# Four graph-attention layers on one core: the last head's norm, scaling and output of a batch written into the next batch's layer 0

## The chip, the core and the metric

The kernel runs on one core of a Trainium2 chip. A core has TensorE (PE; its weight loads are shown apart as PEld), VectorE (DVE), ScalarE (ACT), GpSimd (POOL) and SyncE (SP), and 16 DMA engines that move data between the device memory and the on-chip memories SBUF and PSUM. The metric is the device time of one execution in microseconds (us).

## The reference, cut to what matters

There are 16 batches of 1024 nodes with 256 features, and one 0/1 adjacency matrix of 1024 x 1024 for each batch. Four layers follow one another, and each adds an attention over the graph to x:

```python
h = jnp.maximum(_layernorm(x, axis=-1), 0.0)
x = x + _L0_gnn_ref(h, adj, L0_gnn_W, L0_gnn_a)
...
h = jnp.maximum(_layernorm(x, axis=-1), 0.0)
x = x + _L3_gnn_ref(h, adj, L3_gnn_W, ...)
```

Layers 0 to 2 have one head of 256 features. Layer 3 has H = 4 heads of E = 64 features, and its end is what the change is about; per head and node it is

```python
dst = jnp.einsum('bhij,bhje->bhie', attention, h) + bias[None, :, None, :]
out = jax.nn.relu(dst) + h
mu = out.mean(axis=-1, keepdims=True)
var = out.var(axis=-1, keepdims=True)
out = (out - mu) / jnp.sqrt(var + EPS) * ln_gamma[None, :, None, :] + ln_beta[None, :, None, :]
```

and the four heads side by side are added to x, which is the output.

## The kernel before

**Layout.** A batch's x lies in one tile `x_b` of 128 partitions by 8 row blocks by 256 features. The attention weights of a layer or head are 8 tiles `weights` of 128 x 1024, each built by one VectorE instruction (L318 in `weigh`) from `row`, a PSUM tile that TensorE fills with 8 transposes (L314), and from the adjacency mask. `row` has one buffer for everybody: `weigh` waits in `row_taken` until the one before has built its 8 tiles.

**One layer (`attend`).** The 8 tiles of weights are built while TensorE makes the products (L409) of row blocks 0 and 1 into two PSUM accumulators `acc`. Then each further row block i of 2 to 7 takes 8 products. `finish` reads an accumulator, scales it by the inverse of the row's total (L333, L334) and adds it to x: L449 on VectorE in layer 0, and in layers 1 and 2 `add_elu` with L341 and L343 on ScalarE and L344 and L345 on VectorE. Every second block, `project` begins the next layer for a pair of blocks: mean and centring on VectorE (L271, L274), the squares on ScalarE (L281), the inverse root on GpSimd (L260, L261), the transposes on TensorE (L290), their copy `hT` on ScalarE (L292), the projection on TensorE (L297), and the eviction into `V` (L361, then L363 or L365; for layer 3 L381 and L382 into `h3`, then GpSimd's L384, L388 and L389).

**Layer 3.** For each of the four heads the products (L519) use quarter tiles of TensorE. The sums are copied by ScalarE (L581), transposed (L588, L596), divided by the totals and written to `y` (L599). Then two helpers follow: `center(h)` adds the bias on GpSimd (L487), applies relu and adds h3 (L488), takes the mean (L490, L491), subtracts it (L492), squares on ScalarE (L494), sums the squares (L496) and calls the inverse root on GpSimd (L260, L261); `rescale` multiplies by it on VectorE (L500) and by gamma on GpSimd (L501), and adds x (L502). A head's `rescale` is written behind the next head's L599; that of the last head stands at the end of the batch, with the two output DMAs (L613).

**Order.** The kernel is two Python generators, `stream(0)` over the even batches and `stream(1)` over the odd ones. Each `yield` hands back an estimated duration, and the stream with the smaller sum goes on; the second starts 111 units late, so that one stream is in layer 3 while the other is in layers 0 to 2. This gives the order in which instructions are written. The framework then orders each engine's instructions by that order and by readiness, except where `keep_in_program_order` pins one; it also places tiles in buffers and sets all semaphores. Of the tiles concerned, `y` and `h3` have one buffer for both streams, `x_b` three, `V` four, the accumulators two per stream.

Of the kernel before, what the change touches and what calls it, by code (L numbers as in the profile page):

```python
# [59 lines left out]
def short_path(ctx: ExitStack, tc: tile.TileContext, ins: dict, out: bass.AP, bad: bass.AP):  # L60

    nc = tc.nc
    x, adj = ins["x"], ins["adj"]
    B, N, D = x.shape
    H, T, E = ins["L3_a_src"].shape
    NI = N // P
    NK = D // P
    HALF = 512
    NH = N // HALF
    NG = HALF // P  # L70
# [25 lines left out]
    def in_blocks(a: bass.AP) -> bass.AP:  # L96
        return a.rearrange("(c p t) f -> p c t f", p=P, t=2)
# [166 lines left out]
    def accumulator(b: int) -> bass.AP:  # L264
        return psum.tile([P, HALF], F32, name=f"acc{b % 2}")
# [40 lines left out]
    def weigh(b: int, column, c, op, into: list):  # L306


        while row_taken:
            yield 0.25  # L310
        row_taken.append(b)
        r = psum.tile([P, N], F32, name="row", bufs=1)
        for i in range(NI):
            nc.tensor.transpose(r[:, ts(i, P)], column(i).to_broadcast([P, P]), ident)  # L314
        yield 0.5
        for j in range(NI):
            w = edges.tile([P, N], F32, name=f"weights{b % 2}")
            nc.vector.scalar_tensor_tensor(w, r, c(j), masks[b][:, j // 2, :, j % 2], op0=op, op1=ALU.mult)  # L318
            into.append(w)
            if j == NI - 1:  # L320
                row_taken.pop()
            yield 0.5

    def start(behind, b: int):

        for t in behind:
            if row_taken == [b]:
                return
            yield t
# [16 lines left out]
            xi, above, 0.0, xi, op0=ALU.add, op1=ALU.add, accum_out=total  # L346
        )

    def batch(b: int):
        xb = xs.pop(b)  # L350
        if b == 0:
            next(preparing)
# [40 lines left out]
        def attend(l: int, V: bass.AP, finish, then: int):  # L393

            weights = []
            behind = weigh(
                b, lambda i: V[:, i, D + 2 : D + 3], lambda j: V[:, j, D + 1 : D + 2],
                ALU.min if l == 1 else ALU.max, weights,
            )
            yield from start(behind, b)  # L400
            following = begin(then) if then < 3 else begin3()
            steps = iter(())
            accs = {}
            sums = small.tile([P, NI], F32, name="sums_of_x")

            def product(i: int, j: int):
                if j == 0:
                    accs[i] = accumulator(b)[:, : D + 1]
                nc.tensor.matmul(  # L409
                    accs[i], weights[j][:, ts(i, P)], V[:, j, : D + 1],  # L410
                    start=(j == 0), stop=(j == NI - 1),
                )


            for j in range(NI):
                next(behind)
                product(0, j)
                product(1, j)
                if b == 0 and j == NI - 1:


                    next(preparing)
                    if l == 0:
                        next(loading[1])
                    next(preparing, None)
                yield 0.9
            for _ in behind:
                pass
            for i in range(NI):
                if i > 1:  # L430
                    for j in range(NI):
                        product(i, j)
                acc = accs.pop(i)
                finish(i, acc, sums[:, i : i + 1])
                if i != 0:
                    yield 3.6
                if i % 2 == 1:

                    yield from steps
                    steps = project(b, then, xb, sums, i // 2, following[1])  # L440
                yield from islice(steps, 1)
            yield 1.0
            yield from steps
            return following[0]
# [9 lines left out]
        def finish(i: int, acc: bass.AP, total: bass.AP):  # L454
            add_elu(xb[:, i, :], acc, total)
# [23 lines left out]
        y = single.tile([P, NI, H, E], F32, name="y")  # L479
        normed = []  # L480
        shape = [P, NI, E]

        def center(h: int):

            yh = y[:, :, h, :]
            head = ts(h, E)
            nc.gpsimd.tensor_add(yh, yh, bias[:, head].unsqueeze(1).to_broadcast(shape))  # L487
            nc.vector.scalar_tensor_tensor(yh, yh, 0.0, h3[:, :, head], op0=ALU.max, op1=ALU.add)  # L488
            mean = small.tile([P, NI], F32, name="mean")
            nc.vector.tensor_reduce(mean, yh, AX.X, ALU.add)  # L490
            nc.vector.tensor_scalar_mul(mean, mean, 1.0 / E)  # L491
            nc.vector.tensor_sub(yh, yh, mean.unsqueeze(2).to_broadcast(shape))  # L492
            square = wide.tile(shape, F32, name="wide", bufs=1)
            nc.scalar.activation(square, yh, AF.Square)  # L494
            var = small.tile([P, NI], F32, name="var")
            nc.vector.tensor_reduce(var, square, AX.X, ALU.add)  # L496
            return yh, head, inverse_root(var, NI, E, L3_EPS)

        def rescale(yh: bass.AP, head, rstd: bass.AP):
            nc.vector.tensor_mul(yh, yh, rstd.unsqueeze(2).to_broadcast(shape))  # L500
            nc.gpsimd.tensor_mul(yh, yh, gamma[:, head].unsqueeze(1).to_broadcast(shape))  # L501
            nc.gpsimd.tensor_add(yh, yh, xb[:, :, head])  # L502
# [46 lines left out]
        for h in range(H):  # L549


            acc = accumulator(b)
            total = accumulator(b)
            if h == 0:
                for first in range(0, NI, 4):
                    for _ in range(4):
                        next(behind)
                    pinned = []
                    for j in (first + 2, first):
                        add_values(h, j)  # L560
                    yield 3.6
                for _ in behind:
                    pass
            behind = weigh3(h + 1)
            yield from start(behind, b)

            for first in range(0, NI, 4):
                pinned = []
                for j in (first + 2, first):
                    add_totals(h, j)  # L570
                    if h > 0:
                        add_values(h, j)
                for _ in range(4):
                    next(behind, None)
                yield 1.8 if h == 0 else 5.4
            for _ in behind:
                pass
            copies = []
            for accT in (acc, total) if h == 0 else (total, acc):
                copies.append(wide.tile([P, HALF], F32, name="sums"))  # L580
                nc.scalar.copy(copies[-1], accT)  # L581
                next(testing)
                next(coming, None)
            sums, totals = copies if h == 0 else copies[::-1]
            yield 0.5
            turned = psum.tile([P, NG, P], F32, name="misc")
            for i in range(NG):
                nc.tensor.transpose(turned[:, i, :], totals[:, ts(i, P)], ident)  # L588
            inv = small.tile([P, NH, NG], F32, name="inv8")
            nc.vector.tensor_reduce(  # L590
                inv, turned[:, :, ::QUAD].rearrange("p i (g n) -> p g i n", n=2), AX.X, ALU.add
            )
            inverse(inv, inv)
            turned = psum.tile([P, NG, NH, E], F32, name="misc")
            for i in range(NG):
                nc.tensor.transpose(  # L596
                    turned[:, i].rearrange("p g e -> p (g e)"), sums[:, ts(i, P)], ident
                )
            nc.vector.tensor_mul(  # L599
                y[:, :, h, :].rearrange("p (g i) e -> p g i e", g=NH),  # L600
                turned.rearrange("p i g e -> p g i e"),
                inv.unsqueeze(3).to_broadcast([P, NH, NG, E]),
            )
            yield 0.5
            if h > 0:
                rescale(*normed.pop())
            normed.append(center(h))
            yield 1.0
        for _ in coming:
            pass  # L610
        rescale(*normed.pop())
        for g in range(NH):
            nc.gpsimd.dma_start(  # L613
                in_blocks(out[b, ts(g, HALF), :]),
                y[:, ts(g, NG)].rearrange("p (c t) h e -> p c t (h e)", t=2),
            )
        yield 1.0


    def stream(first: int):  # L620
        for _ in loading[first]:
            yield 2.0
        for b in range(first, B, 2):
            yield from batch(b)

    loading, preparing = [load(0), load(1)], prepare()
    next(loading[0])
# [2 lines left out]
    while streams:  # L630
        ahead = min(streams, key=lambda s: s[0])
        t = next(ahead[1], None)
# [381 lines left out]
```

## Time and profile before

The time before is 2988.73 us, the median of three runs (2987.17 to 2989.75). The span of the profiled execution is 2988.9 us with 44636 instructions.

| what | busy us | share of the span |
|---|---|---|
| TensorE matmuls | 2839.7 | 95% |
| TensorE weight loads | 1986.1 | 66% |
| VectorE | 2148.9 | 72% |
| ScalarE | 1090.0 | 36% |
| GpSimd | 956.7 | 32% |

| group of instructions | count | busy us, mean ns of one |
|---|---|---|
| L409 PE products of layers 0 to 2 | 6144 | 1436.6, 385 |
| L519 PE products of layer 3 | 6144 | 692.1, 597 |
| L318 DVE weights (both forms) | 896 | 1104.2, 1273 and 1275 |
| L488 DVE relu and h3 | 64 | 44.2, 690 |
| L494 ACT squares of a head | 64 | 40.1, 627 |
| L487 POOL bias | 64 | 84.8, 1325 |
| L501 POOL gamma | 64 | 81.4, 1273 |
| L502 POOL adding x | 64 | 83.6, 1307 |
| L613 POOL output DMA issues | 32 | 24.8, 775 |

A matmul's mean of 385 ns is its stay in the pipeline and not the interval between two: a row of 32 of L409 takes 6.93 us. A bracket in a timeline, such as [1.16 <-POOL y L487], is the time for which the engine stood idle just before the instruction, and what ended it.[...]

### The profile page before, as it was taken

What the parts mean: (1) busy time and instruction counts of PE and PEld (TensorE: products, weight loads), DVE (VectorE), ACT (ScalarE), POOL (GpSimd) and SP (SyncE); (2) the same over time, 40 slices, a digit from 0 to 9 for tenths busy, and PEclk for the clock granted to TensorE, in tenths of its full rate; (3) what the DMA queues carried; (4) which work ended last, traced back from release to release, by engine and by line L of the source; (5) the groups of instructions that cost most, each with busy time, mean ns of one, the idle gap of its engine ahead of it and who ended that gap; (6) DMA issues with size and microseconds to landing.
All of it is one profiled execution on the core that took longest, in us unless ns stands there. A gap on an engine that the chain in (4) does not pass through costs nothing.

```text
span 2988.9 us, 44636 instructions
## 1 busy us (share of the span) xinstructions
PE 2839.7 (95%) x16774; PEld 1986.1 (66%) x16774; DVE 2148.9 (72%) x4467; ACT 1090.0 (36%) x3009; POOL 956.7 (32%) x1455
## 2 busy tenths in 40 slices
PE   7999999999999999999999999999999999999985
PEld 5775856768576685766758566685766857667552
DVE  5658688585976859678586885859768586785855
ACT  2333434343343433424334243433434334343331
POOL 2123324243242423424233242432424233242333
PEclk9999999999999999999999999999999999999987
DMA  7204122040221303122041220302213031110101
GB/s 122 39 8 60 33 29 57 8 50 29 30 56 17 55 16 50 36 29 57 5 51 32 29 57 8 50 29 32 55 17 59 11 50 36 15 29 6 25 18 26
DMA packets 120495, 106.11 MB, mean 36 GB/s; under 512 B 73680, under 2 KB 91216, under 8 KB 120272
## 3 DMA queue, kind: packets, MB, share of 16 engines
q0 software_dynamic: 40448, 67.12, 15.4%
q1 hardware_dynamic: 79824, 36.05, 5.8%
q8 instruction: 135, 2.21, 0.3%
q14 instruction: 88, 0.72, 0.1%
HBM read 153.49 MB, written 33.55 MB: 63 GB/s over the span
## 4 chain that ended last, share of the span: by engine, by line
PE 55%; DVE 28%; issue 8%; POOL 5%; ACT 3%; DMA 1%; POOLq 0%; SPq 0%; ACTq 0%; DVEq 0%
PE acc L409 33%; DVE weights L318 19%; PE acc L297 9%; PE acc L519 9%; PE misc L290 2%; POOL rstd L261 2%; POOL y L487 1%; ACT square L281 1%; DVE x_b L345 1%; DVE V L365 1%; PE row L314 1%; DVE x_b L344 1%; ACT below L341 1%; DVE y L488 1%; DVE var L496 1%
## 5 line engine op out<-in xcount | busy, mean ns | idle before, releaser
L409 PE MATMUL acc<-V,weights 128*128 128x257 f32 x6144 | 1436.6, 385 | 26.2 <-DVE weights L318 15.7
L409 PEld LDWEIGHTS acc<-V,weights 128*128 128x128 f32 x6144 | 1143.3, 191 | 262.0 <-DVE weights L318 68.5
L318 DVE SCALAR_TENSOR_TENSOR weights<-row,ex,mask 128x1024 f32<-128x1024 f32 x512 | 630.3, 1273 | 102.5 <-PE row L314 95.7
L519 PE MATMUL acc<-weights,V 128*32 128x512 f32 x6144 | 692.1, 597 | 11.4 <-DVE weights L318 7.5
L297 PE MATMUL acc<-W,hT 128*128 128x259 f32 (+1 forms) x2048 | 521.6, 391 | 40.4 <-ACT hT L292 28.9
L297 PEld LDWEIGHTS acc<-W,hT 128*128 128x128 f32 x2048 | 379.0, 191 | 148.3 <-ACT hT L292 35.1
L318 DVE SCALAR_TENSOR_TENSOR weights<-row,V,mask 128x1024 f32<-128x1024 f32 x384 | 473.9, 1275 | 0.7 <-PE row L314 0.7
L519 PEld LDWEIGHTS acc<-weights,V 128*32 128x32 f32 x6144 | 189.4, 110 | 422.9 <-issue 415.3
L341 ACT ACTIVATE below<-acc,inv 128x256 f32<-128x256 f32 x256 | 120.8, 472 | 798.9 <-DVE inv L334 559.5
L281 ACT ACTIVATE square<-x_b,minus_mean 128x256 bf16<-128x256 f32 x512 | 259.7, 507 | 230.8 <-DVE minus_mean L271 155.0
L261 POOL TENSOR_TENSOR rstd<-rstd,minus_half 128x2 f32<-128x2 f32 (+1 forms) x320 | 302.0, 944 | 20.3
L389 POOL TENSOR_TENSOR x_b<-x_b,beta 128x256 f32<-128x256 f32 x128 | 93.4, 730 | 490.9 <-ACT square L281 490.9
L260 POOL TENSOR_SCALAR rstd<-squared 128x2 f32<-128x2 f32 x256 | 57.7, 225 | 573.2 <-ACT square L281 572.3
L333 DVE TENSOR_SCALAR inv<-acc 128x1 f32<-128x1 f32 x256 | 39.3, 154 | 277.6 <-PE acc L409 276.4
L344 DVE SCALAR_TENSOR_TENSOR x_b<-below,x_b 128x256 f32<-128x256 f32 x256 | 136.8, 534 | 82.7 <-ACT below L341 82.5
L292 ACT ACTIVATE hT<-misc 128x512 f32<-128x512 f32 x256 | 150.0, 592 | 119.9 <-PE misc L290 119.5
L361 ACT ACTIVATE V<-acc,rstd 128x3 f32<-128x3 f32 x384 | 98.5, 262 | 251.7 <-PE acc L297 250.8
L581 ACT COPY sums<-acc 128x512 f32<-128x512 f32 x128 | 74.8, 585 | 278.6 <-PE acc L519 278.6
L365 DVE TENSOR_SCALAR V<-acc,rstd,V 128x256 f32<-128x256 f32 x256 | 131.7, 538 | 62.2 <-ACT V L361 61.3
L290 PE MATMUL misc<-ident,centered 128*128 128x128 f32 x1024 | 158.7, 277 | 15.7 <-DVE centered L274 13.9
L274 DVE TENSOR_SCALAR centered<-x_b,minus_mean 128x256 f32<-128x256 f32 x512 | 168.5, 357 | 5.2
L290 PEld LDWEIGHTS misc<-ident,centered 128*128 128x128 f32 x1024 | 121.3, 141 | 60.1 <-issue 26.9
(76 smaller groups left out, 2218.1 us busy)
## 6 DMA issues: line engine op xcount, KB each, us to landing
adj_i<-in_adj_dram POOLq DMA_DIRECT2D x128, 256.0 KB, 3.9
x_b<-in_x_dram SPq DMA_DIRECT2D x16, 1024.0 KB, 6.4
narrow<-in_adj_dram POOLq DMA_DIRECT2D x64, 256.0 KB, 9.3
out_dram<-y POOLq DMA_DIRECT2D x32, 512.0 KB, 7.4
mask<-narrow SPq DMA_TRANSPOSE x64, 4.4
W<-in_L_gnn_W_dram SPq DMA_DIRECT2D x3, 256.0 KB, 7.2
weights<-in_L_gnn_a_dram SPq DMA_DIRECT2D x3, 256.0 KB, 8.5
W<-in_L_gnn_W_dram SPq DMA_DIRECT2D x2, 128.0 KB, 8.2
```

Source lines behind the costliest of these rows:

```text
L261: nc.gpsimd.tensor_tensor(r, r, minus_half.to_broadcast([P, n]), op=ALU.pow)
L274: nc.vector.tensor_scalar(centered[:, n, :], xb[:, 2 * pair + n, :], minus_mean[:, n : n + 1], 0.0, op0=ALU.add, op1=ALU.max,)
L281: nc.scalar.activation(square, xb[:, 2 * pair + n, :], AF.Square, bias=minus_mean[:, n : n + 1], accum_out=squared[:, n : n + 1],)
L290: nc.tensor.transpose(turned[:, k, ts(n, P)], centered[:, n, ts(k, P)], ident)
L292: nc.scalar.mul(hT, turned, ROOT_D)
L297: nc.tensor.matmul(projected, hT[:, k, ts(n, P)], W[l][:, k, :], start=(k == 0), stop=(k == NK - 1),)
L318: nc.vector.scalar_tensor_tensor(w, r, c(j), masks[b][:, j // 2, :, j % 2], op0=op, op1=ALU.mult)
L341: nc.scalar.activation(below, acc[:, :D], AF.Exp, scale=inv)
L344: nc.vector.scalar_tensor_tensor(xi, below, 1.0, xi, op0=ALU.min, op1=ALU.add)
L365: nc.vector.tensor_scalar(V[:, i, :D], projected[:, :D], rstd, V[:, i, D : D + 1], op0=ALU.mult, op1=ALU.mult,)
L409: nc.tensor.matmul(accs[i], weights[j][:, ts(i, P)], V[:, j, : D + 1], start=(j == 0), stop=(j == NI - 1),)
L519: made = nc.tensor.matmul(accT[ts(n, QUAD), :], values, moving, start=first, stop=last)
```

## The change

`batch` becomes a generator that returns another generator, `ending`. It holds what was at the end of the batch: `center` of the last head, its `rescale`, and the two output DMAs, in three pieces. `stream` hands it to the next `batch` of the same stream, and layer 0's loop over row blocks takes one piece ahead of the products of block 2, one ahead of block 3, one ahead of block 4. The purpose is that this work of VectorE, GpSimd and ScalarE no longer stands between one batch and the next, but beside a run of products. The last batch of each stream has no successor, and there `stream` runs the pieces at once. No instruction is added or left out.

```diff
-    def batch(b: int):
+    def batch(b: int, before):
...
             for i in range(NI):
                 if i > 1:
+                    if l == 0:
+                        yield from islice(before, 1)
                     for j in range(NI):
                         product(i, j)
...
             if h > 0:
                 rescale(*normed.pop())
-            normed.append(center(h))
+            if h < H - 1:
+                normed.append(center(h))
             yield 1.0
         for _ in coming:
             pass
-        rescale(*normed.pop())
-        for g in range(NH):
-            nc.gpsimd.dma_start(
-                in_blocks(out[b, ts(g, HALF), :]),
-                y[:, ts(g, NG)].rearrange("p (c t) h e -> p c t (h e)", t=2),
-            )
-        yield 1.0
+
+        def ending():
+            normed.append(center(H - 1))
+            yield 0.5
+            rescale(*normed.pop())
+            yield 0.5
+            for g in range(NH):
+                nc.gpsimd.dma_start(
+                    in_blocks(out[b, ts(g, HALF), :]),
+                    y[:, ts(g, NG)].rearrange("p (c t) h e -> p c t (h e)", t=2),
+                )
+            yield 0.5
+
+        return ending()
...
+        ending = iter(())
         for b in range(first, B, 2):
-            yield from batch(b)
+            ending = yield from batch(b, ending)
+        yield from ending
```

## The prediction

> **What bounds the kernel now.** I read the page from the busy shares down, then one steady period of the trace. The page's busy part says which engine could be the bound:
>
> ```profile
> PE 2839.7 (95%) x16774; PEld 1986.1 (66%) x16774; DVE 2148.9 (72%) x4467; ACT 1090.0 (36%) x3009; POOL 956.7 (32%) x1455
> ```
>
> TensorE is busy 95% of the span, so only the stretches where it isn't busy can be won. In the chain of waits the 6.96 us "issue" piece returns at 1675.94, 1857.26 and 2038.59 us: the steady state repeats every 181.3 us, once per batch, with the two streams in swapped roles. The windows of one period, 10 us each, show where TensorE has holes (columns: window, length, then busy us of PE, PEld, DVE, ACT, POOL with instruction counts, granted clock, DMA share, GB/s):
>
> ```profile
> 1720.00:1730.00 10.00, 10.00 (x76) 6.11 (x68) 9.97 (x22) 6.50 (x15) 4.50 (x7) 1.00 0.20 30
> 1740.00:1750.00 10.00, 10.00 (x72) 5.51 (x71) 3.35 (x8) 4.76 (x9) 4.61 (x5) 1.00 0.22 30
> 1750.00:1760.00 10.00, 8.90 (x54) 7.26 (x53) 7.86 (x29) 8.45 (x30) 4.51 (x7) 1.00 0.16 25
> 1760.00:1770.00 10.00, 8.53 (x39) 7.00 (x40) 9.09 (x11) 4.20 (x14) 8.10 (x10) 1.00 0.22 57
> 1770.00:1780.00 10.00, 9.88 (x49) 7.90 (x48) 7.48 (x23) 3.60 (x12) 1.76 (x4) 1.00 0.44 154
> ```
>
> Of the 18 windows of the period, 1750 to 1770 holds the largest hole, 1.10 + 1.47 = 2.57 us; elsewhere I find 1.35 us in 1710 to 1720, 0.80 in 1690 to 1700, and under 0.3 in any other. The timeline of VectorE (DVE) says what this place is:
>
> ```profile
> 1753.31 0.68 DVE L599 TENSOR_TENSOR y<-misc,inv 128x512 f32<-128x512 f32 x1
> ...
> 1755.95 0.69 DVE L488 SCALAR_TENSOR_TENSOR y<-y,h 128x512 f32<-128x512 f32 x1 [1.16 <-POOL y L487]
> ...
> 1756.82 0.68 DVE L490 TENSOR_REDUCE mean<-y 128x8 f32<-128x512 f32 x1
> ...
> 1758.01 0.69 DVE L492 TENSOR_TENSOR y<-y,mean 128x512 f32<-128x512 f32 x1
> ...
> 1759.39 0.69 DVE L496 TENSOR_REDUCE var<-wide 128x8 f32<-128x512 f32 x1 [0.24 <-ACT wide L494]
> 1760.00 1.27 DVE L318 SCALAR_TENSOR_TENSOR weights<-row,V,mask 128x1024 f32<-128x1024 f32 x1
> 1762.18 0.69 DVE L500 TENSOR_TENSOR y<-y,rstd 128x512 f32<-128x512 f32 x1 [0.91 <-POOL rstd L261]
> 1762.79 0.54 DVE L365 TENSOR_SCALAR V<-acc,rstd,V 128x256 f32<-128x256 f32 x1
> 1763.25 2.47 DVE L318 SCALAR_TENSOR_TENSOR weights<-row,V,mask 128x1024 f32<-128x1024 f32 x2
> ```
>
> This is the ending of a batch (L599 is its last head; L488 to L500 centre and scale that head), threaded through the first weights (L318) of the other stream's layer 2. The brackets are DVE standing idle for GpSimd (POOL) or ScalarE (ACT). The waits of TensorE in 1751 to 1782:
>
> ```profile
> PE acc L297 <- ACT hT L292: 1.8, 1, 1.8
> PE acc L297 <- DVE V L365: 0.4, 1, 0.4
> PE acc L297 <- ACT above L343: 0.2, 1, 0.2
> ```
>
> **The skill.** "Perfetto Trace Analysis", section "Identifying the Most-Contended Engine", says that matmul busy time misstates TensorE's headroom. The trace agrees here: from 1769.36 the timeline gives 16 products as 4.40 us busy, while 32 of them in the chain take 6.93 us, so 16 cost 3.47; 0.93 us more is lost inside "busy" time. "Trainium Architecture — The Big Picture", section "Inside one NeuronCore", says each engine has its own instruction stream and meets the others only at semaphores; the 0.91 us idle ahead of L500, with weights queued behind it, is what this costs when the order of one stream is unlucky. "SBUF — State Buffer", section "Who interferes with whom", says a GpSimd instruction that reads SBUF and a VectorE one with two SBUF inputs lock each other out for a whole instruction. The trace agrees: L344 takes 0.43 us in most places but 1.45 us at 1731.03, where POOL's L502 runs from 1730.92 to 1732.20.
>
> **What the edit moves, and its size.** No instruction is added or removed. For 14 of the 16 batches (0 to 13; the last of each stream has no next batch) the ending is written later in the program: the centre of head 3 ahead of row block 2 of the next layer 0, the scale ahead of block 3, the output ahead of block 4. Engine order does follow the program only as far as readiness lets it (the next batch's L461 runs at 1711, though written after L599 at 1753), so I read "later" as "behind layer 0's projection, weights and first products when both are ready". The moved work per batch:
> - DVE: L488 0.69, L490 0.68, L491 0.17, L492 0.69, L496 0.69, L500 0.69, together 3.61 us, and the waits 1.16 + 0.24 + 0.91 = 2.31 us.
> - ACT: the square L494, 0.63 us, ahead of which ACT waits 1.06 us for L492.
> - POOL: L487 1.39, L260 0.24, L261 1.65, L501 1.26, L502 1.27 and the two output issues 1.55, together 7.36 us.
> - The output transfer (7.4 us to landing) and the fetch of x_b, which comes at 1766.08 just as L502 frees its slot. Both stay hidden: the fetched x_b is first summed 126 us later (L461 at 1711 plus a period), and y is next written by the other stream at L599, 1682 plus a period, 97 us later.
>
> **What the old place gains.** Two chains. First, the transposes L290 end at 1759.11, but ACT's copy L292 starts only at 1760.40, behind two squares L281 and one L361 that queued behind L494. Without L494 these three (0.6 + 0.26 + 0.6 = 1.45 us) start where ACT went idle, 1757.67, and end about 1759.1; L292 starts about 1759.3, and TensorE resumes 1.1 us earlier. Second, the eight weights run from 1760.00 to 1772.58. Without the ending they could start at about 1759.15 (the last row transpose ends at 1758.34, then an L365 of 0.53), and they need 8 x 1.2 + 2.0 (four L365 of about 0.5) = 11.6 us, hence end at about 1770.7: 1.8 us earlier; where L365 also runs before the row is complete, 1770.1, or 2.5 us. TensorE's own work from 1759.1 to the end of these products (32 of L409 at 0.217, 16 of L297 at 0.222, 4 transposes at 0.11) is 10.9 us against 14.7 elapsed, so from 1759.95 it could end at 1770.9. Both chains allow some 2.5 us; the most there is to win is the hole and the hidden 0.93, 3.4 us. I take 2.5.
>
> **What the new place costs.** Layer 0's blocks 2 to 4 come at about 1792 to 1805. There TensorE has no hole at all, and VectorE and GpSimd are half free:
>
> ```profile
> 1792.00:1837.00 45.00, 45.00 (x223) 39.19 (x222) 17.53 (x68) 17.88 (x56) 15.63 (x33) 1.00 0.00 1
> ```
>
> So the 3.6 us of DVE work fits by volume. It can still delay: a DVE instruction waiting for POOL holds what is queued behind it, here L333/L334 and L449 or L344/L345, which free the accumulators (two per stream), and L274, which feeds the transposes. TensorE can absorb about one stream's 16 products, 3.5 us, since the two streams alternate. Lower end of the cost: 0, as every gap is filled. Upper end: the two POOL waits (up to 2.1 us each, as the wait 1740.86 for L261 shows) and three lock-outs of about 0.8 us (L344's 1.45 less 0.43, and 0.67 at 1696.90), some 6.6 us of DVE delay, of which half passes the cushion, 3.3. I take 0.8.
>
> Net: (2.5 - 0.8) x 14 = 23.8 us, so 2988.7 - 23.8 = 2965 us.
>
> **The rivals.**
> 1. Full recovery: the ending vanishes into the 45 us where DVE is 39% busy, and the whole hole closes, 3.2 x 14 = 45, to 2944 us. For it: DVE waits there 18.8 us for TensorE (L333 10.2 + 8.6). Against: the POOL share of DVE's lock-outs.
> 2. The wait moves: slower. h3 has one buffer for both streams. The other stream's first write of h3 (L382) is at 1791.35, and the last read of the old h3 is L488 in the ending. Before, L488 was at 1755.95, 35 us clear. If the centre really goes behind L449 of block 0 (1792.58), L487 and L488 (1.39 + 0.69) end at about 1795, and ACT's L382 with everything queued behind it slips by some 3.5 us, holding the accumulators of the projection. Gain 2.5, cost 3.5: (1.0) x 14 = +14, 3003 us. Against it: the ending's inputs are ready from 1754, DVE has holes before 1791 in which it may be placed, and L382 is written about as late as the centre.
> 3. Nothing moves: readiness places the ending in the same holes, 1754 to 1766, as now; 2989 us, give or take the reshuffling of the rest (6 us). For it: the weights it should yield to are not ready before 1758.
>
> **The numbers.** Forecast 0.45, full recovery 0.17, wait moved 0.24, nothing moves 0.14. Faster by over 0.2% (6 us): the first two and a third of the last, 0.67; same 0.07; slower 0.26. The range reaches from full recovery to the moved wait, 2943 to 3003; what lies beyond is about half of the slower case and a little of the fast one.
>
> **What would show it.** Right: the period falls from 181.3 to about 179.6; between a batch's last L599 and the other stream's eight L318 stand no L488 to L500; TensorE's wait for L292 of 1.8 us and the pieces around the weights shrink; windows 1792 to 1837 keep TensorE near 100%. The cost term is wrong if new waits of L297 or L409 appear among layer 0's blocks. Rival 2 shows as ACT's L382 waiting for L488, rival 3 as L488 to L500 still within 13 us of L599. The forecast is wrong if the hole closes and a hole of its size opens elsewhere in the period.

## The result, and the profile after

The changed kernel takes 3034.86 us, the median of six runs (3033.95 to 3036.61); the kernel before took 2987.9 (2987.1 to 2989.75) beside it. The ratio is 1.0157, with a 95% interval of 1.0144 to 1.017: slower by 47 us, where 2965 was forecast and 3003 was the upper end. In its file before's L487 to L502 have become L491 to L506, L599 is L603, L613 is L623, L409 is L411, L519 is L523, L361 to L365 are L363 to L367, and L381 and L382 are L383 and L384; the files of the experiments have the same, up to a few lines further down.

The busy part of the page after:

```profile
PE 2856.3 (94%) x16774; PEld 1990.5 (66%) x16774; DVE 2168.0 (71%) x4467; ACT 1092.8 (36%) x3009; POOL 960.1 (32%) x1455
```

The counts are those of before, and each engine's busy time has grown by 20 us at most, while the span grew by 44. TensorE has 17 us more of busy time and 28 more of idle time, so most of what was added is waiting. The steady state has changed its shape too. Before, a batch came every 181.3 us and all were alike. Now the last L603 of batches 2, 4, 6 and 8 stands at 680.02, 1053.29, 1426.37 and 1798.03 us: a pattern of two batches that takes 373.3, 373.1 and 371.7, or 186.3 per batch. The two halves differ: 168 us to the end of an odd batch, 205 to the end of an even one. The windows around the end of an odd batch (window, length, busy us of PE, PEld, DVE, ACT, POOL, granted clock, that is the share of full speed at which TensorE's clock ran, DMA share, GB/s):

```profile
1200.00:1210.00 10.00, 8.26 (x66) 3.92 (x66) 5.59 (x20) 7.43 (x21) 3.21 (x6) 1.00 0.64 116
1210.00:1220.00 10.00, 9.09 (x43) 7.50 (x43) 5.74 (x10) 2.40 (x6) 5.67 (x6) 1.00 0.28 42
1220.00:1230.00 10.00, 8.54 (x44) 7.22 (x44) 8.69 (x30) 7.57 (x25) 4.91 (x8) 1.00 0.01 2
1230.00:1240.00 10.00, 8.60 (x40) 7.21 (x41) 5.38 (x17) 5.82 (x21) 7.03 (x8) 1.00 0.25 67
1240.00:1250.00 10.00, 8.48 (x44) 6.46 (x42) 6.36 (x8) 3.13 (x9) 0.84 (x2) 1.00 0.37 145
```

TensorE has holes of 7.03 us in these 50 us, in every window. VectorE's timeline of the same place:

```profile
1197.69 2.46 DVE L318 SCALAR_TENSOR_TENSOR weights<-row,ex,mask 128x1024 f32<-128x1024 f32 x2
...
1221.39 0.68 DVE L603 TENSOR_TENSOR y<-misc,inv 128x512 f32<-128x512 f32 x1
1225.26 0.68 DVE L492 SCALAR_TENSOR_TENSOR y<-y,h 128x512 f32<-128x512 f32 x1
...
1228.84 0.69 DVE L500 TENSOR_REDUCE var<-wide 128x8 f32<-128x512 f32 x1 [0.95 <-ACT wide L498]
1231.73 0.69 DVE L504 TENSOR_TENSOR y<-y,rstd 128x512 f32<-128x512 f32 x1
...
1245.82 9.63 DVE L318 SCALAR_TENSOR_TENSOR weights<-row,V,mask 128x1024 f32<-128x1024 f32 x8 [1.57 <-PE row L314]
```

Two things are to be seen. The ending (L492 to L504) is still within 11 us of the last L603: it did not go to layer 0's row blocks. And from 1200.15 to 1245.82, for 45.7 us, no weights are built at all. In the kernel before, the timeline has the pause between the weights of the last head and the next layer's as

```profile
1363.69 2.47 DVE L318 SCALAR_TENSOR_TENSOR weights<-row,ex,mask 128x1024 f32<-128x1024 f32 x2
1397.32 1.27 DVE L318 SCALAR_TENSOR_TENSOR weights<-row,V,mask 128x1024 f32<-128x1024 f32 x1
```

that is, from 1366.16 to 1397.32, 31.2 us. The two streams no longer meet as they did. Why they don't, and whether this is the whole of the loss, is what the experiments ask.

### The profile page after: what moved, and what is told of

Read it like the earlier page. It is cut to its first block, busy times and chain, and to the rows that moved or that the text cites. A ratio compares the mean times of both kernels' runs of the same rounds, so it can differ in the third digit from the quotient of the medians.

```text
span 3033.2 us, 44574 instructions
## 1 busy us (share of the span) xinstructions
PE 2856.3 (94%) x16774; PEld 1990.5 (66%) x16774; DVE 2168.0 (71%) x4467; ACT 1092.8 (36%) x3009; POOL 960.1 (32%) x1455
## 5 line engine op out<-in xcount | busy, mean ns | idle before, releaser
L411 PE MATMUL acc<-V,weights 128*128 128x257 f32 x6144 | 1434.8, 385 | 37.6 <-DVE weights L318 12.2
L411 PEld LDWEIGHTS acc<-V,weights 128*128 128x128 f32 x6144 | 1146.2, 191 | 275.1 <-DVE weights L318 66.6
L523 PE MATMUL acc<-weights,V 128*32 128x512 f32 x6144 | 694.2, 599 | 15.9 <-DVE weights L318 14.3
L318 DVE SCALAR_TENSOR_TENSOR weights<-row,ex,mask 128x1024 f32<-128x1024 f32 x512 | 629.7, 1274 | 62.0 <-PE row L314 53.4
L297 PE MATMUL acc<-W,hT 128*128 128x259 f32 (+1 forms) x2048 | 529.0, 395 | 53.0 <-ACT hT L292 30.3
L318 DVE SCALAR_TENSOR_TENSOR weights<-row,V,mask 128x1024 f32<-128x1024 f32 x384 | 468.9, 1275 | 27.1 <-PE row L314 27.0
L523 PEld LDWEIGHTS acc<-weights,V 128*32 128x32 f32 x6144 | 190.0, 110 | 430.7 <-issue 424.3
L281 ACT ACTIVATE square<-x_b,minus_mean 128x256 bf16<-128x256 f32 x512 | 260.2, 508 | 383.1 <-DVE minus_mean L271 317.4
L341 ACT ACTIVATE below<-acc,inv 128x256 f32<-128x256 f32 x256 | 120.6, 472 | 678.2 <-DVE inv L334 448.4
L260 POOL TENSOR_SCALAR rstd<-squared 128x2 f32<-128x2 f32 x256 | 66.1, 258 | 773.1 <-ACT square L281 771.7
L261 POOL TENSOR_TENSOR rstd<-rstd,minus_half 128x2 f32<-128x2 f32 (+1 forms) x320 | 296.6, 927 | 21.2
L367 DVE TENSOR_SCALAR V<-acc,rstd,V 128x256 f32<-128x256 f32 x256 | 134.3, 539 | 86.8 <-ACT V L363 86.2
L274 DVE TENSOR_SCALAR centered<-x_b,minus_mean 128x256 f32<-128x256 f32 x512 | 185.3, 402 | 4.7
L344 DVE SCALAR_TENSOR_TENSOR x_b<-below,x_b 128x256 f32<-128x256 f32 x256 | 124.0, 486 | 80.7 <-ACT below L341 79.6
L290 PE MATMUL misc<-ident,centered 128*128 128x128 f32 x1024 | 157.4, 278 | 21.6 <-DVE centered L274 21.3
L363 ACT ACTIVATE V<-acc,rstd 128x3 f32<-128x3 f32 x384 | 99.2, 261 | 213.9 <-PE acc L297 212.2
L290 PEld LDWEIGHTS misc<-ident,centered 128*128 128x128 f32 x1024 | 122.5, 142 | 67.3 <-DVE centered L274 20.1
```

The source lines that it names most:

```text
L261: nc.gpsimd.tensor_tensor(r, r, minus_half.to_broadcast([P, n]), op=ALU.pow)
L274: nc.vector.tensor_scalar(centered[:, n, :], xb[:, 2 * pair + n, :], minus_mean[:, n : n + 1], 0.0, op0=ALU.add, op1=ALU.max,)
L281: nc.scalar.activation(square, xb[:, 2 * pair + n, :], AF.Square, bias=minus_mean[:, n : n + 1], accum_out=squared[:, n : n + 1],)
L290: nc.tensor.transpose(turned[:, k, ts(n, P)], centered[:, n, ts(k, P)], ident)
L297: nc.tensor.matmul(projected, hT[:, k, ts(n, P)], W[l][:, k, :], start=(k == 0), stop=(k == NK - 1),)
L341: nc.scalar.activation(below, acc[:, :D], AF.Exp, scale=inv)
```

## The experiments

The change does two things that are easily taken for one. It **moves the work**, and it **changes the turns**: the `yield 1.0` at the end of a batch is dropped and three of 0.5 are put into layer 0, so each batch counts for 0.5 units more, and its layer 0 starts one unit earlier after the batch ahead of it. (The recorded expectations call the sum of the yields the clock; TensorE's granted clock is another thing.) The turns decide which stream gets the one `row` buffer next. Adding up the yields of the code gives the order in which the layers and heads take it (L2.4 is layer 2 of batch 4, h2.3 is head 2 of batch 3, @ the stream's sum):

```
before  h0.3@505.6 h1.3@512.8 L1.4@518.0 h2.3@524.4 h3.3@537.2 L2.4@567.4 L0.5@579.8 h0.4@616.8 h1.4@624.0 L1.5@629.2
change  h0.3@500.1 h1.3@507.3 h2.3@512.9 L1.4@525.7 h3.3@532.2 L0.5@573.8 L2.4@580.1 L1.5@624.7 h0.4@631.0 h1.4@638.2
```

Before, the order is the same for every batch: layer 2, layer 0 of the other stream, heads 0 and 1, layer 1, heads 2 and 3. With the turns of the change, of some 15 such places, layer 0 goes ahead of layer 2 in 7, layer 1 behind head 2 in 7 and ahead of head 0 in 7. In the last three of the 7 (after batches 9, 11 and 13) layer 1 goes behind head 3 as well, and there the trace's pattern changes again: the last three pairs of batches take 375.0, 365.1 and 364.3 us. So within one run another order of `row` goes with another period. Layer 1 and layer 2 belong to the same stream, so if head 2 goes first, only one head is left to be worked on beside layer 1. The pause of 45.7 us above is such a place: ahead of it the timeline has the weights of layer 1 up to 1184.26 and then those of one head, where the kernel before has those of two heads between layer 1 and the pause.

The theories: A, the turns cost the time. B, the moved work does. For how the work could cost it there were three: W, a new wait of the multiply L504 for GpSimd; H, h3 held too long (the prediction's second rival); P, any disturbed order costs.

**Work or turns.** The first run keeps the change's place and restores the turns of before; the second keeps the work where it was and takes the turns of the change.

```diff
+++ e1_work_moved_old_clock (against the change)
-            yield 0.5
+            yield 0.0
...
+        yield 1.0
         return ending()
+++ e2_old_place_new_clock (against before; layer 0 takes the pieces as in the change)
-        yield 1.0
...
+        def ending():
+            yield 0.5
+            yield 0.5
+            yield 0.5
+        return ending()
```

> The ending is written inside the next layer 0 as in the change, but its three pieces yield 0 and the yield of 1.0 at the end of a batch is kept, so that adding up the yields gives the two streams the same turns as before the change. Theory A (turns): the loss comes from the yields, which let layer 0 of an odd batch take the row buffer ahead of layer 2 of the other stream; with the old turns the time is back at 2988, within 15 us, with one period per batch of about 181 us. Theory B (moved work): the loss comes from the work in its new place (VectorE and GpSimd waits there, or h3 with its one buffer); then it stays, 3020 to 3040.

> The kernel before, with the ending in its old place, but with the yields of the change: no yield of 1.0 at the end of a batch, and three empty yields of 0.5 ahead of blocks 2, 3 and 4 of the next layer 0. The two streams then take turns as in the change. Theory A (turns): about 3035, 3015 to 3050, with a pattern that repeats every two batches. Theory B (moved work): as before, 2988 within 6 us.

e1 took 3029.85 us (1.0133, 1.0116 to 1.015), e2 3037.74 (1.0162, 1.0145 to 1.0179), beside 2989.33. Each part alone costs nearly what the whole change costs, so A and B both hold. They don't add: the turns are worth 48 in the old place, but only 5 on top of e1.

**Other turns.** Two more settings of the yields, each with the work in the new and in the old place: 1.5 units more per batch than before, and 1.0 less (there the edit is made to all three yields).

```diff
+++ e3_change_plus_end_yield (against the change)
+        yield 1.0
         return ending()
+++ e4_change_no_yields (against the change)
-            yield 0.5
+            yield 0.0
+++ e13_old_place_clock_of_e3 (against e2)
+        yield 1.0
         return ending()
+++ e12_old_place_no_end_yield (against e2)
-            yield 0.5
+            yield 0.0
```

> The change with the yield of 1.0 at the end of a batch put back, the pieces still yielding 0.5 each: 1.5 more per batch than before. Adding up the yields, layer 2 of the other stream again takes the row buffer ahead of every layer 0, as before the change. Theory A (turns): within 20 us of 2988. Theory B (moved work): 3020 to 3040, since the work is where the change has it.

> The change with its pieces yielding 0 and no yield at the end of a batch: 1.0 less per batch than before. Adding up the yields, the order in which layers take the row buffer is again that of before. Theory A (turns): within 20 us of 2988. Theory B (moved work): 3020 to 3040.

> The kernel before with the clock of e3 (0.5 more ahead of each of blocks 2, 3, 4 of layer 0, the yield at the end kept). Here layer 1 takes row after head 2 instead of head 1 in 7 of 15 places, the rest as before. This is what the expectation of e3 overlooked. Theory A (order of row): slower than before by the part of e3's 90 us that its 40 us of moved work don't explain, so 3020 to 3050. If the order of row doesn't matter: 2989 within 10 us.

> The kernel before without the yield of 1.0 at the end of a batch and nothing else (the clock of e4, the ending in its old place). The order of row is that of before. Theory A read as 'the order of row decides': within 12 us of 2989. If any other clock costs: 3005 or more.

e3 took 3079.41 (1.03, 1.0283 to 1.0317), e4 3013.87 (1.0082, 1.0065 to 1.0099), e13 3054.79 (1.0222, 1.0205 to 1.0239) and e12 2998.52 (1.0032, 1.0021 to 1.0042). The expectation for e3, within 20 us of 2988 or 3020 to 3040, missed: I had looked only at layers 0 and 2, which keep their order there, and not at layer 1, which goes behind head 2 in 7 of 15 places. e4 came out between its two ranges, and e13 5 us above its own. Layer 1's place is the only difference of e13's order of `row` from before's, and e13 costs 65 us without any work moved. In e12 the order is before's in every place, and the cost is 9.1 beside 2989.41, as was expected if the order of `row` decides. This speaks for the order of `row` as the larger part of what the yields do, but it doesn't show it: each setting also shifts the finer order of writing, by another amount.

**What in the moved work costs.** Two runs with e1's turns move less of it: e7 leaves the centre of head 3 in its old place and moves only its `rescale` and the output, e8 only the output.

```diff
+++ e7_centre_stays (against e1)
-            if h < H - 1:
-                normed.append(center(h))
+            normed.append(center(h))
...
-            normed.append(center(H - 1))
+++ e8_only_output_moved (against e7)
+        rescale(*normed.pop())
...
-            rescale(*normed.pop())
```

> Turns of before; the centre of the last head is written at its old place, only its rescale and the output are written inside the next layer 0. Theory W: the sum of squares is early again, so the multiply by the root can't stand waiting in front of add_elu; 2975 to 2995. Theory P: 3005 to 3040. Theory H says the same as W here, about 2988.

> Turns of before; only the two output DMAs are written inside the next layer 0. No engine but GpSimd sees a difference (1.55 us of issue). Theories W and H: as before, 2988 within 6 us. Theory P: slower by more than 6 us.

e7 took 2989.77 (1.0006, 0.9997 to 1.0015), e8 2989.22 (1.0001, 0.9992 to 1.0009). The output and its slot of `x_b` cost and gain nothing, and moving the multiply with them leaves the time as it was: only with the centre moved does the time go up. Nor does P hold as a rule, since both runs disturb the order. VectorE's timeline of e1 shows how:

```profile
1412.46 0.69 DVE L496 TENSOR_TENSOR y<-y,mean 128x512 f32<-128x512 f32 x1
...
1420.84 3.66 DVE L318 SCALAR_TENSOR_TENSOR weights<-row,V,mask 128x1024 f32<-128x1024 f32 x3
...
1426.11 0.68 DVE L500 TENSOR_REDUCE var<-wide 128x8 f32<-128x512 f32 x1
1426.70 0.21 DVE L334 RECIPROCAL inv<-inv 128x1 f32<-128x1 f32 x2
1428.89 0.69 DVE L504 TENSOR_TENSOR y<-y,rstd 128x512 f32<-128x512 f32 x1 [1.98 <-POOL rstd L261]
1429.50 0.42 DVE L344 SCALAR_TENSOR_TENSOR x_b<-below,x_b 128x256 f32<-128x256 f32 x1
1430.03 1.30 DVE L345 SCALAR_TENSOR_TENSOR x_b<-above,x_b 128x256 f32<-128x256 f32 x1
...
1431.26 1.47 DVE L344 SCALAR_TENSOR_TENSOR x_b<-below,x_b 128x256 f32<-128x256 f32 x1
...
1433.91 0.38 DVE L271 TENSOR_SCALAR minus_mean<-sums_of_x 128x2 f32<-128x2 f32 x1
...
1436.84 1.27 DVE L318 SCALAR_TENSOR_TENSOR weights<-row,V,mask 128x1024 f32<-128x1024 f32 x1
```

The last head's L603 was at 1407.59 and its mean was subtracted at 1412.46, but the sum of squares L500 has fallen behind the other stream's eight weights, to 1426.11. The multiply L504 follows behind it on VectorE, with only two short reciprocals between, and waits there 1.98 us for GpSimd's L260 and L261. Queued behind it is the first `add_elu` of the other stream's layer 2, whose L344 starts at 1429.50 though ScalarE's L341, which it reads, had ended at 1427.42. When the multiply is done, GpSimd starts on L505 (1429.66) and L506 (1431.12), and beside these L345 takes 1.30 and L344 1.47 us. The multiply's wait of 0.91 us in the kernel before had weights behind it. Here it also has the centring L271 and L274 of the other stream's next projection behind it, and TensorE waits for that, as the waits of e1 from 1425 to 1440 say:

```profile
PE misc L290 <- DVE centered L274: 2.3, 1, 2.3
DVE y L504 <- POOL rstd L261: 2.0, 1, 2.0
```

**Take the wait away.** `keep_in_program_order` pins the multiply of the last head to where it is written, ahead of layer 0's block 3; nothing else in the program differs from e1. GpSimd's L505 and L506, which need its result, go with it. e9 pins the first VectorE instruction of the centre (L492) as well, so that the whole ending goes to layer 0.

```diff
+++ e6_scale_pinned (against e1)
-            nc.vector.tensor_mul(yh, yh, rstd.unsqueeze(2).to_broadcast(shape))
+            scaled = nc.vector.tensor_mul(yh, yh, rstd.unsqueeze(2).to_broadcast(shape))
+            if pin:
+                tc.keep_in_program_order(scaled)
...
-            rescale(*normed.pop())
+            rescale(*normed.pop(), pin=True)
+++ e9_all_pinned (against e6)
-            nc.vector.scalar_tensor_tensor(yh, yh, 0.0, h3[:, :, head], op0=ALU.max, op1=ALU.add)
+            added = nc.vector.scalar_tensor_tensor(yh, yh, 0.0, h3[:, :, head], op0=ALU.max, op1=ALU.add)
+            if pin:
+                tc.keep_in_program_order(added)
...
-            normed.append(center(H - 1))
+            normed.append(center(H - 1, pin=True))
```

> As e1_work_moved_old_clock (ending written in the next layer 0, turns of before), but the VectorE multiply of the ending's rescale (L504 there) is pinned to its written place, so it no longer stands ahead of the first add_elu of the other stream's layer 2, where it waited 1.98 us for GpSimd in e1. Theory W (the new wait of this multiply is the loss): the hole of TensorE behind it (2.3 us of L290 waiting for L274) closes, and the time falls from 3030 to 2975 to 2990. Theory H (h3 is held too long): no change, since the centre stays where it was; 3025 to 3035. Theory P (any disturbed order costs): 3005 to 3040.

> As e6, and the first VectorE instruction of the ending's centre (the relu with h3) is pinned as well, so the whole ending really runs at blocks 2 and 3 of layer 0. Now the last read of h3 comes after about 1792 in the period of the kernel before, where the other stream first writes h3 at 1791.35. Theory H (h3 with one buffer holds the other stream): ScalarE's write of h3 waits for that read, and TensorE loses 2 to 4 us per batch against e6, so 20 to 60 us above e6. Theory W: as e6 or up to 15 us below it, since VectorE has 39% load there.

e6 took 2965.93 us (2962.93 to 2966.42; 0.9919, 0.9903 to 0.9936) and e9 2949.91 (2947.51 to 2950.72; 0.9866, 0.985 to 0.9883), beside 2988.73. One pinned instruction is worth 64 us, and e9 beats both kernels, by 38.8 and by 85. For e6 theory W had expected 2975 to 2990, so the pin gained more than the wait had cost. The timeline of e6, in which the multiply has gone to where the program has it:

```profile
1398.54 0.68 DVE L500 TENSOR_REDUCE var<-wide 128x8 f32<-128x512 f32 x1
1399.13 0.21 DVE L334 RECIPROCAL inv<-inv 128x1 f32<-128x1 f32 x2
1399.89 0.43 DVE L344 SCALAR_TENSOR_TENSOR x_b<-below,x_b 128x256 f32<-128x256 f32 x1 [0.54 <-ACT below L341]
1400.42 0.42 DVE L345 SCALAR_TENSOR_TENSOR x_b<-above,x_b 128x256 f32<-128x256 f32 x1
...
1402.56 0.16 DVE L271 TENSOR_SCALAR minus_mean<-sums_of_x 128x2 f32<-128x2 f32 x1
...
1405.34 1.28 DVE L318 SCALAR_TENSOR_TENSOR weights<-row,V,mask 128x1024 f32<-128x1024 f32 x1
...
1430.58 0.69 DVE L504 TENSOR_TENSOR y<-y,rstd 128x512 f32<-128x512 f32 x1
```

From L500 to L271 it is 4.02 us, where e1 had 7.80. The pin takes away more than the wait: up to the first L344 it saves 2.04 us (3.39 less 1.35: the wait and the multiply itself, less the 0.54 that e6 waits for ScalarE), and the other 1.74 lie between there and L271, where L345 and L344 no longer run beside GpSimd. No run takes away one of these without the other. What this does to TensorE, in 10 us windows from the last L603 on; first e1, then e6:

```profile
1407.59:1417.59 10.00, 8.52 (x48) 7.18 (x47) 9.86 (x19) 8.42 (x30) 6.01 (x11) 1.00 0.01 2
1417.59:1427.59 10.00, 10.00 (x49) 8.39 (x47) 8.85 (x15) 2.03 (x6) 0.69 (x3) 1.00 0.00 0
1427.59:1437.59 10.00, 7.71 (x36) 6.22 (x34) 7.71 (x16) 3.65 (x12) 7.40 (x9) 0.87 0.35 85
1437.59:1447.59 10.00, 10.00 (x45) 8.27 (x44) 9.89 (x14) 0.84 (x2) 0.61 (x1) 0.96 0.32 127
```

```profile
1380.05:1390.05 10.00, 8.53 (x48) 7.19 (x47) 9.86 (x19) 8.41 (x30) 6.03 (x11) 1.00 0.01 2
1390.05:1400.05 10.00, 10.00 (x49) 8.37 (x47) 8.98 (x16) 2.05 (x6) 0.69 (x3) 1.00 0.00 0
1400.05:1410.05 10.00, 9.94 (x51) 8.34 (x51) 8.44 (x20) 3.84 (x12) 3.75 (x5) 1.00 0.00 1
```

The first 20 us are equal to within 0.01 us of TensorE. The third window is short by 2.29 us in e1 and by 0.06 in e6. In e1 the granted clock also falls to 0.87 and 0.96, which would be another 1.3 + 0.4 = 1.7 us of TensorE. But the fall isn't what costs the time. In the batch that ends at 1776.94 the clock stays at 1.00, and there TensorE stands still a second time, for the weights:

```profile
1804.08 0.70 PE L290 MATMUL misc<-ident,centered 128*128 128x128 f32 x4 [2.29 <-DVE centered L274]
...
1807.51 7.70 PE L411 MATMUL acc<-V,weights 128*128 128x257 f32 x34 [1.43 <-DVE weights L318]
```

From 1776.94 to the next batch's last L603 (1960.55) it is 183.61 us, against 183.67 after 1407.59, where the clock fell for about 3 us: the slower products only fill the time until VectorE has the weights ready. What e1 loses is VectorE's delay. From L500 to the first weights of the next layer 0 (L318) it takes 10.73 us in e1 and 6.80 in e6, a difference of 3.93, and the periods, 183.67 (from 1407.59 to 1591.26) and 179.6 (1380.05 to 1559.65), differ by 4.07. In 4 of e1's batches the clock stays at one half for nearly 7 us, and only these periods are longer, 185.7 to 185.8. So ten batches at 4.0 and four at 6.1 make the 64 us.

The same measure serves for all runs with before's turns. Counted from a batch's last L603 (at 1753.31 in before, where it is L599, at 1570.96 in e7, 1407.59 in e1, 1380.05 in e6 and 1551.32 in e9), the other stream's eight weights for layer 2 end, and the first weights for the next layer 0 begin, at (us):

| run | eight weights end | next weights begin | period | period less that beginning |
|---|---|---|---|---|
| before | 19.27 | 27.02 | 181.32 | 154.30 |
| e7 | 17.67 | 27.16 | 181.45 | 154.29 |
| e1 | 16.91 | 29.25 | 183.67 | 154.42 |
| e6 | 16.88 | 25.29 | 179.60 | 154.31 |
| e9 | 16.05 | 23.85 | 178.57 | 154.72 |

The last column is the same to within 0.5 us. So apart from e1's long falls of the clock, nearly all that these kernels differ by lies between the last head and the next layer 0. It also shows what e7 hides: without the multiply the eight weights end 1.6 us earlier, and behind them the multiply, with L344 and L345 slowed beside GpSimd, gives it all back. So W in a wider sense, the multiply ahead of `add_elu` with its wait and with what GpSimd does behind it, accounts for the loss of e1.

e9 also tests H, since there the old h3 is really read late. The timeline of ScalarE and VectorE, then one of the waits from 1400 to 1430, in e9:

```profile
1407.27 0.27 ACT L383 ACTIVATE ex<-acc,rstd 128x12 f32<-128x12 f32 x1 [1.02 <-PE acc L297]
...
1410.55 0.68 DVE L492 SCALAR_TENSOR_TENSOR y<-y,h 128x512 f32<-128x512 f32 x1
1411.49 0.82 ACT L384 ACTIVATE h<-acc,rstd 128x256 f32<-128x256 f32 x2
```

```profile
PEld acc L411 <- ACT h L384: 0.5, 1, 0.5
```

The write of h3 (L384) stands some 4 us later than right behind its L383, just after the read L492 has ended at 1411.23. ScalarE isn't shown waiting; the write was placed behind the read. So the dependence that rival 2 named is there, and its delay has the size that rival 2 gave it, but it costs TensorE 0.5 us, not 3.5: ScalarE does four squares (L281) meanwhile, and TensorE's window from 1402.56 to 1412.56 still has 9.88 us busy. The table's last column has 0.4 us more for e9 than for e6. H had expected 2 to 4 us per batch.

**The two faults together.** The pin in the change itself, with its own turns, and in e4, with 1.0 unit less per batch than before.

```diff
+++ e10_change_scale_pinned (against the change), e11_no_yields_scale_pinned (against e4)
-            rescale(*normed.pop())
+            rescale(*normed.pop(), pin=True)
```

> The change with its own yields, and the ending's multiply pinned as in e6_scale_pinned. The wait ahead of add_elu is gone, the turns are those of the change (7 of 15 times layer 0 of the next batch takes row before layer 2 of the other stream, 7 times layer 1 takes it after head 2, 7 times before head 0). Theory A (turns cost apart from the wait): the 48 us of e2 on top of e6, 2995 to 3020. Theory W alone (the wait is all there is): near e6, 2960 to 2975.

> As e6_scale_pinned, without the yield at the end of a batch (the clock of e4: 1.0 less per batch). The order in which layers and heads take the row buffer is that of before in every place. Theory A read as 'the order of row decides': e4's 3014 less the 64 us that the pin gave between e1 and e6, so 2950 to 2975. If any other clock than the old one costs, whatever the order of row: 2985 or more.

e10 took 3009.76 us (1.0071, 1.0054 to 1.0088) and e11 2989.73 (1.0003, 0.9994 to 1.0012), beside 2989.41. So all settings stand like this (us; "units" are those of a batch against before's; before itself took 2987.9 to 2989.41 beside the several runs):

| work and pin | turns of before | of the change (+0.5 units) | -1.0 units | +1.5 units |
|---|---|---|---|---|
| old place | 2988.73 | 3037.74 (e2) | 2998.52 (e12) | 3054.79 (e13) |
| moved | 3029.85 (e1) | 3034.86 (the change) | 3013.87 (e4) | 3079.41 (e3) |
| moved, multiply pinned | 2965.93 (e6) | 3009.76 (e10) | 2989.73 (e11) | |
| moved, centre pinned too | 2949.91 (e9) | | | |

Once the wait is gone, the turns cost 3009.76 - 2965.93 = 44 us, close to the 48 of the old place. With the pin the two parts of the change add: -23 for the move and +48 for the turns make +25, and +20 was measured. e11 came out as its second alternative, 2985 or more if any other sum of yields costs whatever the order of `row`: it has before's order in every place and is still 24 us above e6. So with the pin another sum of the yields costs more than half of those 44 us without any change in the order of `row`.

The pinned centre with the change's turns was not tried, nor was a second buffer of h3.

## Why the prediction was wrong

**What held.** The hole of the old place and its causes. e9 is the kernel that the forecast describes, with the whole ending beside layer 0's products. There the eight weights end 3.2 us earlier, where I had taken 2.5 for the gain, and the first window after the last L603 holds 9.62 us of TensorE,

```profile
1372.56:1382.56 10.00, 9.62 (x53) 8.13 (x52) 8.72 (x16) 7.96 (x30) 6.05 (x11) 1.00 0.01 2
```

where before had in the same place

```profile
1390.63:1400.63 10.00, 7.78 (x43) 6.20 (x41) 7.65 (x19) 8.33 (x30) 7.48 (x11) 1.00 0.01 2
```

Its period is 178.6 us, a gain of 2.7 per batch (where I had taken 0.8 for the cost of the new place, the table's last column has 0.4), and its 2950 us are nearer to the "full recovery" of rival 1, 2944, than to the forecast. e6 has the very numbers of the forecast, a period of 179.6 and 2965.9 us against 2965, but in it the centre stands within 5 us of the last L603, ahead of the weights, and only the multiply is in layer 0. That it agrees to 1 us is luck. That the output and the fetch of `x_b` stay hidden held in e8. So the gain was to be had, but not in the kernel that was to be run.

**First step that failed: "I read 'later' as 'behind layer 0's projection, weights and first products when both are ready'."** The trace has the multiply 10 us behind the last L603 in odd batches (1231.73 after 1221.39), 17 in even ones (1070.67 after 1053.29) and 21 in e1, which is near rival 3's placement and far from the 50 us of e6, where it is in layer 0. I had named the evidence myself (L461 runs at 1711, ahead of what is written before it) and then costed only the place in which the program has the work. Freed from its old place, the ending was not placed later but re-sorted among the other stream's weights and `add_elu`. The term "I take 0.8" was the cost of a place where it never was, and rival 3, "give or take the reshuffling of the rest (6 us)", had nearly the right placement, with the wrong cost. The wait and the slow instructions beside GpSimd were in my text as an upper end: "the two POOL waits ... some 6.6 us of DVE delay, of which half passes the cushion, 3.3". Net of the old hole's gain, that end would have been 2.5 - 3.3, or +11 us in all. In e1 the cost was 4.07 us per batch beyond e6, and 6.1 in the batches with the long fall of the clock, since it came where TensorE's next projection and the next weights hung on VectorE, and not where 45 us of products were queued.

**Second step that failed, by being left out: the yields.** The sum has no term for them. I described them in the section on the kernel as an estimated duration that decides which stream goes on, and treated the change from 1.0 to three of 0.5 as bookkeeping. e2 alone, with no work moved, costs 48 us. It could have been worked out blind: adding up the yields needs only the code, and the table of turns shows layer 0 overtaking layer 2. Its size could not.

**In the change itself** both faults are there: the pin takes 25 us off (e10), before's turns alone take 5 (e1), both together take 69 (e6). So without the pin the two hide behind each other. The group of the multiply, in the page's form (after the bar: busy us, mean ns, idle us before it and what ended it), shows the wait in the kernel before, in the changed kernel and with the pin, e10:

```profile
L500 DVE TENSOR_TENSOR y<-y,rstd 128x512 f32<-128x512 f32 x64 | 43.9, 687 | 49.7 <-POOL rstd L261 49.7
```

```profile
L504 DVE TENSOR_TENSOR y<-y,rstd 128x512 f32<-128x512 f32 x64 | 43.9, 687 | 58.8 <-POOL rstd L261 58.5
```

```profile
L504 DVE TENSOR_TENSOR y<-y,rstd 128x512 f32<-128x512 f32 x64 | 43.8, 684 | 37.3 <-POOL rstd L261 37.3
```

The idle time grows by 9.1 us with the change and falls by 21.5 with the pin. So the amount of waiting is not the point: most of it was there before, and in the change's even batches it stands ahead of `add_elu` (1.77 us at 1070.67, with an L345 of 1.30 behind it). Over the 1500 us from 250 to 1750, windows of 10 us give TensorE 45.1 us of holes before and 62.1 after, and a loss by the clock (one less the granted clock, times the length) of 3.4 and 8.5. That is 22 us together, and 1.57% of 1500 is 24. This account is rough: for e1 it gives 30 where the time is 20 longer.

**What stays open.** Which of the three flips of `row` costs how much, and whether the flips do it: e13 has one of them alone, in 7 places, and costs 65, but its yields differ otherwise too. Why e4, e11 and e12, with before's order of `row`, are 9 to 24 us from their neighbours with before's turns: the turns also shift the order within a layer, and no run separates this. And why the two faults don't add when nothing is pinned. How the loss by the moved multiply divides into its wait and GpSimd's work beside `add_elu` is open too.

## What to carry to other kernels

Where a scheduler orders instructions by readiness, moving a piece in the program only says where it may go: look for where its inputs are ready, cost that place, and pin the instruction that would wait for another engine ahead of work that matters more (here one multiply, 64 us). Where two streams are interleaved by counted durations, each yield is part of the schedule: move work and its units separately, work out the order of the shared buffer from the code before measuring, and judge a move only with the old order kept.

## What the runs showed that was not expected

- A hole of TensorE of 2.29 us was followed by a clock of one half. The windows of 1 us in e1 where L290 had waited for L274:

```profile
1432.00:1433.00 1.00, 0.45 (x5) 0.20 (x2) 1.00 (x2) 0.00 (x0) 0.70 (x2) 1.00 0.00 0
1433.00:1434.00 1.00, 0.00 (x0) 0.00 (x0) 1.00 (x5) 0.00 (x0) 1.00 (x2) 1.00 0.75 49
1434.00:1435.00 1.00, 0.27 (x2) 0.21 (x3) 0.96 (x4) 0.60 (x2) 0.29 (x1) 1.00 0.61 135
1435.00:1436.00 1.00, 1.00 (x6) 0.91 (x5) 0.17 (x2) 0.99 (x4) 0.29 (x2) 0.54 0.73 264
1436.00:1437.00 1.00, 1.00 (x4) 0.82 (x3) 0.99 (x2) 0.83 (x2) 1.00 (x2) 0.50 0.94 258
```

  It is 0.50 from just after the hole until 1438.5, and a batch later from 1619.4 to 1626. After the same hole near 1802 it stays at 1.00, as after those near 696 and 1249. The Trainium skill, "TensorE: Matmul & The Clock Gate", section "Part 1: The HAM clock gate (the "warmup" mystery)", gives these two states and says that TensorE falls to half rate after an idle window of about 3.4 us which isn't tied to the program's start. The trace agrees in the two states and in their irregular coming; here a hole of 2.3 us was enough in two of these three batches. Over 250 to 1750 us the loss by the clock is 18.9 us in e1, and 3.4 in before, e6 and e9. Little of it reached the time: the fall of about 3 us left the period where it is without a fall, 183.67 and 183.61, and the one of nearly 7 us added 2.0. A loss by the clock is a cost only as far as TensorE would not have waited anyway.
- VectorE beside GpSimd's L505 and L506 is slowed by more than the prediction's 0.8 us each: L345 1.30 and L344 1.47 us against 0.42. In e9 two L274, which take 0.62 us where nothing runs beside them (1402.75 in e6), took 2.73 us together beside the same work of GpSimd:

```profile
1423.07 2.73 DVE L274 TENSOR_SCALAR centered<-x_b,minus_mean 128x256 f32<-128x256 f32 x2
```

  That was amid layer 0's products, where TensorE didn't miss them: the window from 1422.56 to 1432.56 has it busy for 10.00 us.
- In e7 the multiply fell behind the weights by itself and waited for nothing, and its old wait of 0.91 us was gone. The weights ended 1.6 us earlier, but behind the multiply L344 and L345, beside GpSimd, took 0.95 and 1.29 us instead of 0.42, the next weights began 0.1 us later than before, and the time was the same to 0.06%: a wait that goes from the brackets gains nothing if its engine pays for it further down.
